# Sums over the states in a selective scan: two blocks at a time in four column tiles, with smaller rings of buffers

## The chip, the cores and the metric

The kernel runs on one core of a Trainium2 chip. A core has five engines that work side by side, each through its own queue of instructions in order: TensorE (PE in the profile, its weight loads PEld), VectorE (DVE), ScalarE (ACT), GpSimd (POOL) and SyncE (SP), which here issues nearly all DMAs. They wait for each other through semaphores. The metric is the time of one launch on the device in microseconds (us), median of several runs.

## What is computed

The input is a batch of 32 images of 96 channels and 56 x 56 pixels, all in float32. First comes a block of a depthwise 7 x 7 convolution, a layer norm over the channels, two dense layers with a GELU between them, and a residual. Then come two layers of a state space model over the 3136 pixels of an image as a sequence, each of this form:

```python
xs, z = jnp.split(layernorm(seq) @ in_w, 2, axis=-1)       # 192 channels each
xc = silu(causal_conv(xs) + conv_b)
dt, Bm, Cm = split(xc @ xproj_w)                            # 6, 16 and 16 columns
delta = softplus(dt @ dt_w + dt_b)
dA  = exp(delta[..., None] * A)                             # tokens x 192 x 16 states
dBx = delta[..., None] * Bm[:, :, None, :] * xc[..., None]
h   = associative_scan(dA, dBx)                             # h = dA * h_before + dBx
y   = einsum('blds,bls->bld', h, Cm) + Dp * xc              # the sum over the 16 states
seq = seq + (y * silu(z)) @ out_w
```

A fusion with a pooled vector, a batch norm over all images and a residual end it. The change concerns the line of `y`: the sum over the 16 states of each channel.

## The kernel before, in words

**Stages.** An image is cut into 4 chunks of 784 tokens. One chunk in one layer is a stage, 256 in all; the two layers alternate, the second one chunk behind the first. A stage has 24 steps: block `j` (0 to 5) of 32 channels, and in it group `g` (0 to 3) of 4 states. A step's tile has 128 partitions, 4 states x 32 channels, and 784 tokens.

**A step.** ScalarE makes the factor `exp(delta * A)` (L836). For blocks 0, 1, 3 and 4, TensorE spreads the product `delta * xc` of 32 channels onto 128 partitions in PSUM (the spread, L851, once a block, ahead of the block's first step), VectorE multiplies it by B (L878) and scans (L885). For blocks 2 and 5, the constant `POOLED`, GpSimd does that product from a copy in SBUF instead (L862), some steps in advance. Then GpSimd multiplies the states by C (L889) into the tile `da`, and TensorE adds up the four states of a tile with a matrix of ones, `ssum` (L922), in float32. Such a matmul has 128 rows and 32 columns of the array, and the profile has two passes of it.

**The sums.** The tokens of a tile are two halves `a` of 392, and the result `y` of two blocks shares one PSUM tile of 128 partitions: row `64 * a + 32 * (j % 2)`. Each of these four places is a column tile of the array of its own. A step's sum fills two of them. For each pair of blocks a matmul with a diagonal matrix opens the accumulation with `D * xc` (L916), and when the pair is done VectorE multiplies `y` by the gate `z` (L903) and so frees the one buffer of `y`.

**The order of the work** is written by hand. Each engine runs its instructions in the order in which the program issues them. A loop over steps `n` issues the exponentials of a later step, the scan of `n`, at the end of a block the spread of `n + 1`, and the sums of step `n - 3` (`LAG = 3`). Two of the steps (`LATE`) shift the sums by one, so that the opening matmul of the next pair comes behind the gate. All the other work of neighbouring stages is put into numbered slots of the same loop (`put`, `run`), by lists of (slot, piece): the norms (centring L355, mean L365, the multiplies L419 and L575), dense layers and projections (L424, L439, L443, L587, L614, L644), the output projection of the stage before (L750, L756), and in stages 2 to 145 seven taps twice of the convolution of later images (L506). A piece with `True` is issued just ahead of the scan. In the loop of a slot, the spread comes first, the sums next, the pieces last.

**Buffers.** Tiles of one tag form a ring: a new tile takes the place of an old one, and its first writer waits until the old one's last reader is done. The ring `da` of 11 holds the exponentials of blocks 0, 1, 3 and 4 and the products of blocks 2 and 5; each is overwritten by the product with C and read by the sum. B and C of a stage are four tiles `bc`, one a group, in a ring of 8: two stages. Each is loaded by four DMAs (L632), which spread a row over 32 partitions.

Of the kernel before, what the change touches and what calls it, by code (L numbers as in the profile page):

```python
# [34 lines left out]
F32 = mybir.dt.float32  # L35
# [13 lines left out]
NG = 4  # L49
# [3 lines left out]
CH = L // NCH  # L53
HC = CH // 2
# [7 lines left out]
def convnext_mamba_kernel(  # L62
# [31 lines left out]
    nc = tc.nc  # L94
# [34 lines left out]
    for a in range(2):  # L129
        r = slice(64 * a, 64 * a + 64)  # L130
# [8 lines left out]
    ssum = const.tile([128, 32], F32, name="ssum")  # L139
# [55 lines left out]
    for i in range(2):  # L195
# [39 lines left out]
        for s in range(4):  # L235
            r = slice(32 * s, 32 * s + 32)
# [11 lines left out]
    for k in range(2):  # L248
        t = const.tile([C + 1, 3 + CH], F32, name=f"hn{k}", tag=f"hn{k}")
        nc.vector.memset(t[C : C + 1, :], 1.0)  # L250
        hns.append(t)
        t = const.tile([C + 1, HC], F32, name=f"hz{k}", tag=f"hz{k}")
# [7 lines left out]
    with tc.tile_pool(name="cc", bufs=1) as cc, tc.tile_pool(name="cx", bufs=3) as cx, tc.tile_pool(  # L260
        name="cp", bufs=6, space=PSUM
# [4 lines left out]
        for dh in range(7):  # L266
            m = cc.tile([R2, R2], F32, name="m", tag="m", bufs=2)
# [25 lines left out]
        for i in range(3):  # L293
            t = cc.tile([R2, 7, R2], F32, name=f"band{i}", tag=f"band{i}")
            nc.gpsimd.memset(t, 0.0)
            bands.append(t)
            t = cc.tile([R2, b0, W + 6], F32, name=f"xpad{i}", tag=f"xpad{i}")
            nc.gpsimd.memset(t, 0.0)
            xpads.append(t)
        for p in range(C // 2):  # L300
# [13 lines left out]
            for lo in range(0, b0, GB):  # L314
                n = min(GB, b0 - lo)
                ps = cps.tile([R2, GB * W], F32, name="ps")
                for dw in range(7):
                    nc.tensor.matmul(
                        ps[:, 0 : n * W], T[:, dw, :], xp[:, lo : lo + n, dw : dw + W],
                        start=(dw == 0), stop=(dw == 6),  # L320
# [8 lines left out]
    with ExitStack() as main:  # L329
        wp = main.enter_context(tc.tile_pool(name="wp", bufs=2))  # L330
# [12 lines left out]
        def tok(a):  # L343
            return slice(a * HC, (a + 1) * HC)

        def rows(a):
            return slice(64 * a, 64 * a + 64)
# [193 lines left out]
        def prep(S):  # L541
# [52 lines left out]
            def silu(name, bias):  # L594
                def piece():
                    t = wp.tile(
                        [128, NQ, HC], F32, name=name, tag=name, bufs=3 if name == "z" else 2
                    )
                    for q in range(NQ):
                        nc.scalar.activation(  # L600
                            t[:, q, :], v["x", q][:, 0:HC], AF.Silu,
                            bias=0.0 if bias is None else bias[:, q, :],
                        )
                    if name == "z":
                        exp_ln_tables()
                    setattr(S, name, t)

                return piece
# [18 lines left out]
            def load_bc(gs):  # L627
                def piece():
                    for g in gs:
                        t = wp.tile([128, 2, CH], F32, name="bc", tag="bc", bufs=8)  # L630
                        for s in range(4):
                            nc.sync.dma_start(  # L632
                                t[32 * s : 32 * s + 32],
                                v["bd"][4 * g + s :: NS, :].partition_broadcast(32),
                            )
                        S.bcs.append(t)

                return piece
# [54 lines left out]
            def load_d4(j):  # L693
# [11 lines left out]
            start = [  # L705
                (-18, load), (-12.9, center), (-11.9, square), (-11.8, halo), (-11.6, mean),
                (-11.2, root), (-9, True, norm),
            ]
            t = (-7.6, -7.5, -6.5, -6, 0, 0.1, 1, 2.3, 3.1, 3.4, 4)
            if S in (stages[2], stages[-1]):  # L710

                start = [
                    (10.3, center), (10.4, square), (10.5, halo), (10.9, mean), (11, root),
                    (12, norm),
                ]
                t = (12, 12, 13, 13, 14, 14, 15, 16, 17, 18, 19)
            elif S is stages[3]:

                start = [
                    (-18, load), (-4.5, center), (-4.4, square), (-4.3, halo), (-3.5, mean),  # L720
                    (-3, root), (-2, norm),
                ]
                t = (0, 0, 0.1, 0.2, 0.3, 1, 2, 3.3, 4.1, 4.4, 5)
            t = [k + 0.1 for k in t]
# [4 lines left out]
                (t[6], silu("xc", d["cb"])), (t[6] + 0.1, project(0, wz, (0,), 3, 0)),  # L729
                (t[6] + 0.1, project(1, wz, (0,), 3, 0)), (t[6] + 0.1, project(2, wz, (0,), 3, 0)),  # L730
                (t[6] + 0.2, silu("z", None)), (t[7], dbl), (t[8], dbl_out),
                (max(10.2, t[8] + 1.2), load_bc((0, 1))), (max(13.2, t[8] + 2.2), load_bc((2, 3))),
                (t[9], dt), (t[10], softplus),
                (max(16.9, t[10] + 1.5), product(0, 2)), (max(18.3, t[10] + 3.1), store_u(0)),
                (25.2, product(2, 3)), (26.3, store_u(1)),
# [66 lines left out]
        NSTEP = 2 * NQ * NG  # L802

        ring = wp.tile([128, NG, CH], F32, name="h", tag="h", bufs=1)
        LAG = 3
        LATE = (4, 12)
# [8 lines left out]
        for i, b, c in order:  # L815
            S = Stage()
# [5 lines left out]
        def wide():  # L822

            return pu.tile([128, 1024], F32, name="w", tag="w", bufs=2)

        def exps(n):

            m, r = divmod(n, NSTEP)
            if m == len(stages):
                return  # L830
            S, j, g = stages[m], r // NG, r % NG
            if j in POOLED:
                e = wide()[:, 0:CH]
            else:
                e = S.da[j, g] = wp.tile([128, CH], F32, name="da", tag="da", bufs=11)
            nc.scalar.activation(e, S.d4[j], AF.Exp, scale=S.d["A"][:, j, g : g + 1])  # L836
            S.e[j, g] = e

        def lead(n):

            return 1 if n % NSTEP // NG in POOLED else 2

        def spread(n):

            m, r = divmod(n, NSTEP)
            if m == len(stages) or r // NG in POOLED:
                return
            S, j = stages[m], r // NG
            S.u4 = wide()
            for a in range(2):  # L850
                nc.tensor.matmul(  # L851
                    S.u4[:, 512 * a : 512 * a + HC], sel[rows(a), j % 2, :],
                    S.u[rows(a), j // 2, :], start=True, stop=True,
                )

        def pooled(m, j, g):


            def piece():
                S = stages[m]  # L860
                t = S.da[j, g] = wp.tile([128, CH], F32, name="da", tag="da", bufs=11)
                nc.gpsimd.tensor_tensor(t, S.us[j], S.bcs[g][:, 0, :], ALU.mult)  # L862

            return piece
# [26 lines left out]
        def keep_state(n):  # L891

            m, r = divmod(n, NSTEP)
            S, j, g = stages[m], r // NG, r % NG
            if g % 2 == 1 and S.c < NCH - 1:
                nc.scalar.copy(  # L896
                    S.d["st"][:, j, g - 1 : g + 1].unsqueeze(2), ring[:, g - 1 : g + 1, CH - 1 : CH]
                )

        def gate(n):  # L900
            m, r = divmod(n, NSTEP)
            S, q = stages[m], r // NG // 2
            nc.vector.tensor_tensor(S.z[:, q, :], S.y[:, 0:HC], S.z[:, q, :], ALU.mult)  # L903

        def add_up(n):

            if n < 0:
                return
            m, r = divmod(n, NSTEP)
            S, j, g = stages[m], r // NG, r % NG  # L910
            q = j // 2
            if j % 2 == 0 and g == 0:
                if j == 4:
                    gate(n - 1)
                S.y = py.tile([128, 512], F32, name="y", tag="y")
                nc.tensor.matmul(  # L916
                    S.y[:, 0:HC], S.d["D"][:, q, :], S.xc[:, q, :], start=True, stop=False
                )
            da = S.da.pop((j, g))
            for a in range(2):  # L920
                r0 = 64 * a + 32 * (j % 2)
                nc.tensor.matmul(  # L922
                    S.y[r0 : r0 + 32, 0:HC], ssum, da[:, tok(a)],
                    start=False, stop=(g == NG - 1),
                )


        slots, within = {}, {}
# [6 lines left out]
        def run(n, where):  # L935
            for _, piece in sorted(where.pop(n, ()), key=lambda p: p[0]):
                piece()
# [24 lines left out]
        with tc.manual_schedule(  # L962
            engines={ET.PE, ET.Activation, ET.DVE, ET.Pool, ET.SP}
        ):
            end = len(stages) * NSTEP
            for n in range(-2 * NSTEP, 0):
                run(n, within)
                run(n, slots)
            spread(0)
            for n in range(2):  # L970
                exps(n)
            for n in range(end + NSTEP):
                if n < end:
                    for k in (1, 2):
                        if lead(n + k) == k:
                            exps(n + k)
                    if n:
                        keep_state(n - 1)
                    scan(n)
                    if n % NG == NG - 1:  # L980
                        spread(n + 1)
                if n < end + LAG:
                    if n % NSTEP in LATE:
                        add_up(n - LAG - 1)
                    if n % NSTEP + 1 not in LATE:
                        add_up(n - LAG)
                elif n == end + LAG:
                    gate(end - 1)
                if n >= end:
                    run(n, within)  # L990
                run(n, slots)
# [4 lines left out]
    with tc.tile_pool(name="sp", bufs=1) as sp:  # L996
        n = B * NCH
# [21 lines left out]
    with tc.tile_pool(name="fin", bufs=4) as fin:  # L1019
        for b in range(B):  # L1020
            for a in range(2):
# [3 lines left out]
                r = fin.tile([C, 2 * CH], F32, name="fr")  # L1025
# [63 lines left out]
```

## Time and profile before

| | before |
|---|---|
| time, median of 3 runs | 17439.26 us (17436.45 to 17451.02) |
| profiled execution, span | 17444.6 us |
| scans L885, busy | 11076.0 us over four forms of operands, 6144 of them, 1766 to 1844 ns each |
| products L878 of VectorE, busy | 3996.2 us, 976 ns each |
| multiplies by C L889 of GpSimd, busy | 11267.2 us, 1856 ns each |
| products L862 of GpSimd, busy | 3819.1 us, 1865 ns each |
| sums L922 of TensorE, busy | 5147.1 us, 24576 passes |
| bytes moved | 2346 MB, 135 GB/s on average |

How to read it: busy time is the time in which an engine worked on instructions of a group; passes of matmuls overlap, so their mean duration times their number is more than the busy time. The waits of an engine are the times in which it stood idle, put down to what it waited for last. The windows and timelines show short stretches, with the clock granted to TensorE as a share of full speed (1.00 or 0.50).

### The profile page before, as it was taken

Reading aid. Unit: us, or ns where it says so; the run is one execution under the profiler, and the core shown is the slowest. Engines: PE = TensorE matmul, PEld = TensorE weight load, DVE = VectorE, ACT = ScalarE, POOL = GpSimd, SP = SyncE. Lnnn points to the kernel's source line nnn. Section 1 sums busy time; section 2 is a strip of 40 time slices with the busy share of each in tenths; the row PEclk is TensorE's granted clock in tenths of the full one; section 3 lists DMA queues with packets and bytes.
Section 4 is the critical chain, followed back from the end, with each engine's and each line's share of the span. In section 5 each row is a group of like instructions: output and inputs, shape, how many; then the busy total and the mean of one; then the engine's idle time right before and its main releaser. Section 6 shows DMA issues by size and latency. Waiting matters only on the chain. (4 is left out here: it accounts for less than half of the span.)

```text
span 17444.6 us, 217495 instructions
## 1 busy us (share of the span) xinstructions
PE 15502.9 (89%) x67992; PEld 5472.5 (31%) x67992; DVE 16064.8 (92%) x12345; ACT 11460.0 (66%) x18647; POOL 15605.6 (89%) x8737
## 2 busy tenths in 40 slices
PE   7799999999999999999999988888888888888870
PEld 5233333333333333333333322222222222222220
DVE  7499999999999999999999999999999999999994
ACT  1566766666666666666666666666666666666653
POOL 0499999999999999999999999999999999999991
PEclk9799999999999999999999999999999999999985
DMA  4355555555555555555555555555555555555548
GB/s 101 87 141 138 141 138 136 138 140 139 140 135 139 138 139 139 136 137 138 139 140 138 134 126 130 127 125 126 126 129 128 125 126 126 129 127 124 127 115 276
DMA packets 1421981, 2346.44 MB, mean 135 GB/s; under 512 B 629958, under 2 KB 793586, under 8 KB 1420820
## 3 DMA queue, kind: packets, MB, share of 16 engines
q1 hardware_dynamic: 1413652, 2294.00, 53.7%
q10 hardware_dynamic: 7168, 38.54, 0.6%
q8 instruction: 536, 8.78, 0.2%
q14 instruction: 625, 5.12, 0.1%
HBM read 1929.11 MB, written 402.41 MB: 134 GB/s over the span
## 5 line engine op out<-in xcount | busy, mean ns | idle before, releaser
L889 POOL TENSOR_TENSOR da<-h,bc 128x784 f32<-128x784 f32 x6144 | 11267.2, 1856 | 855.6 <-DVE h L885 734.9
L885 DVE TENSOR_TENSOR_SCAN h<-da,st,w 128x784 f32<-128x784 f32 x3072 | 5664.5, 1844 | 326.4 <-ACT st L896 8.6
L922 PE MATMUL y<-da,ssum 128*32 128x392 f32 x24576 | 5147.1, 542 | 407.2 <-POOL da L889 403.2
L878 DVE TENSOR_TENSOR w<-w,bc 128x784 f32<-128x784 f32 x4096 | 3996.2, 976 | 300.9 <-PE w L851 132.7
L862 POOL TENSOR_TENSOR da<-us,bc 128x784 f32<-128x784 f32 x2048 | 3819.1, 1865 | 2.3 <-DMA us<-uu 2.3
L836 ACT ACTIVATE da<-d,A 128x784 f32<-128x784 f32 x4096 | 3757.4, 941 | 43.1 <-DMA d<-dd 27.3
L836 ACT ACTIVATE w<-d,A 128x784 f32<-128x784 f32 x2048 | 1878.3, 918 | 2635.0 <-DVE h L885 2285.8
L885 DVE TENSOR_TENSOR_SCAN h<-w,st,da 128x784 f32<-128x784 f32 x1536 | 2712.2, 1827 | 5.9 <-ACT w L836 4.8
L587 PE MATMUL ps<-hn,wx 97*64 97x392 f32 x12288 | 2265.9, 503 | 7.4 <-DVE hn L575 7.4
L922 PEld LDWEIGHTS y<-da,ssum 128*32 128x32 f32 x24576 | 1094.8, 115 | 3681.1 <-issue 2141.1
L885 DVE TENSOR_TENSOR_SCAN h<-da,w 128x784 f32<-128x784 f32 x1024 | 1827.0, 1784 | 109.1 <-ACT st L896 4.3
L851 PE MATMUL w<-u,sel 64*128 64x392 f32 x4096 | 1026.5, 580 | 655.0 <-DVE h L885 654.0
L587 PEld LDWEIGHTS ps<-hn,wx 97*64 97x64 f32 x12288 | 793.7, 137 | 1434.5 <-issue 1117.3
L666 POOL TENSOR_TENSOR u<-dl,xc 128x784 f32<-128x784 f32 (+1 forms) x512 | 737.5, 1440 | 564.1 <-ACT dl L652 564.1
L916 PE MATMUL y<-xc,D 128*128 128x392 f32 x1536 | 802.2, 608 | 257.1 <-DVE z L903 249.4
L506 PE MATMUL ps<-xpad,band 112*112 112x224 f32 (+1 forms) x4032 | 1003.0, 358 | 0.0
L351 ACT ACT_TABLE_LOAD x759 | 973.8, 1283 | 14.3 <-PEq L1076 0.8
L885 DVE TENSOR_TENSOR_SCAN h<-w,da 128x784 f32<-128x784 f32 x512 | 872.3, 1766 | 0.0
L360 ACT ACTIVATE sq<-ps 96x392 f32<-96x392 f32 x768 | 340.7, 490 | 797.3 <-PE ps L355 448.9
L506 PEld LDWEIGHTS ps<-xpad,band 112*112 112x112 f32 x4032 | 583.7, 175 | 832.5 <-issue 770.0
L644 PE MATMUL ps<-dbl,dtw 6*64 6x392 f32 x3072 | 685.7, 509 | 99.6 <-ACT dbl L622 99.6
L851 PEld LDWEIGHTS w<-u,sel 64*128 64x128 f32 x4096 | 327.9, 196 | 1255.6 <-DVE h L885 1096.3
(124 smaller groups left out, 14444.6 us busy)
## 6 DMA issues: line engine op xcount, KB each, us to landing
bc<-bd SPq DMA_DIRECT2D x4096, 196.0 KB, 5.3
d<-dd SPq DMA_DIRECT2D x6144, 98.0 KB, 2.9
us<-uu SPq DMA_DIRECT2D x2048, 98.0 KB, 2.2
dd<-dl SPq DMA_DIRECT2D x512, 294.0 KB, 3.8
uu<-u SPq DMA_DIRECT2D x1024, 49.0 KB, 1.6
band<-band_d SPq DMA_DIRECT2D x144, 343.0 KB, 3.6
cv<-conv_d SPq DMA_DIRECT2D x256, 147.0 KB, 2.5
xin<-in_x SPq DMA_DIRECT2D x128, 294.0 KB, 4.2
```

Of the source, the lines that this page charges most:

```text
L351: nc.scalar.preload_act_table_set("natural_log_exp_and_others")
L506: nc.tensor.matmul(v["ps"][0:R2, 0 : (last - first) * W], v["band"][:, dw, :], xpad[:, first:last, dw : dw + W], start=(dw == 0), stop=(dw ...
L587: nc.tensor.matmul(v["x", q][rows(a), 0:HC], weights[:, k, 64 * q : 64 * q + 64], v["hn"][:, o : o + HC], start=(k == 0), stop=(k == last),)
L666: nc.gpsimd.tensor_tensor(S.u[:, lo:hi], v["dl"][:, lo:hi], S.xc[:, lo:hi], ALU.mult)
L836: nc.scalar.activation(e, S.d4[j], AF.Exp, scale=S.d["A"][:, j, g : g + 1])
L851: nc.tensor.matmul(S.u4[:, 512 * a : 512 * a + HC], sel[rows(a), j % 2, :], S.u[rows(a), j // 2, :], start=True, stop=True,)
L862: nc.gpsimd.tensor_tensor(t, S.us[j], S.bcs[g][:, 0, :], ALU.mult)
L878: nc.vector.tensor_tensor(halves(db), S.u4.rearrange("p (a b) -> p a b", a=2)[:, :, 0:HC], halves(S.bcs[g][:, 0, :]), ALU.mult,)
L885: nc.vector.tensor_tensor_scan(ring[:, g, :], S.e.pop((j, g)), db, 0.0 if c == 0 else d["st"][:, j, g : g + 1], ALU.mult, ALU.add,)
L889: nc.gpsimd.tensor_tensor(da, ring[:, g, :], S.bcs[g][:, 1, :], ALU.mult)
L916: nc.tensor.matmul(S.y[:, 0:HC], S.d["D"][:, q, :], S.xc[:, q, :], start=True, stop=False)
L922: nc.tensor.matmul(S.y[r0 : r0 + 32, 0:HC], ssum, da[:, tok(a)], start=False, stop=(g == NG - 1),)
```

## The change

The sums of two blocks are done together. In the odd block of a pair, the sum of step `n` takes the tile of the same group of the even block with it: four matmuls in four column tiles instead of two in two, and none during the even block. The opening matmul with `D * xc` moves to the odd block's first sum, the `LATE` shift falls away, and the gate of the second pair is issued at step 19, where it stood before.

The tiles of the even block must live longer, until the odd block's sum. For that the ring `da` of 11 becomes two: 8 tiles for the exponentials of blocks 0, 1, 3 and 4, and a ring `dp` of 6 for the products of blocks 2 and 5. The room comes from B and C: 6 tiles instead of 8, so that the loads of the groups 2 and 3 are issued in slots 22 and 23 of the stage before, where the tiles of the groups 0 and 1 come free, instead of slot 13.

It is meant to make better use of the array[...] and to take half of the bursts of sums off TensorE's queue.

```diff
-                        t = wp.tile([128, 2, CH], F32, name="bc", tag="bc", bufs=8)
+                        t = wp.tile([128, 2, CH], F32, name="bc", tag="bc", bufs=6)
...
-                (max(10.2, t[8] + 1.2), load_bc((0, 1))), (max(13.2, t[8] + 2.2), load_bc((2, 3))),
+                (max(10.2, t[8] + 1.2), load_bc((0, 1))), (22, load_bc((2,))), (23, load_bc((3,))),
...
-                e = S.da[j, g] = wp.tile([128, CH], F32, name="da", tag="da", bufs=11)
+                e = S.da[j, g] = wp.tile([128, CH], F32, name="da", tag="da", bufs=8)
...
-                t = S.da[j, g] = wp.tile([128, CH], F32, name="da", tag="da", bufs=11)
+                t = S.da[j, g] = wp.tile([128, CH], F32, name="da", tag="dp", bufs=6)
...
         def add_up(n):
 
-            if n < 0:
+            m, r = divmod(n, NSTEP)
+            if n < 0 or r // NG % 2 == 0:
                 return
-            m, r = divmod(n, NSTEP)
             S, j, g = stages[m], r // NG, r % NG
             q = j // 2
-            if j % 2 == 0 and g == 0:
-                if j == 4:
-                    gate(n - 1)
+            if g == 0:
                 S.y = py.tile([128, 512], F32, name="y", tag="y")
                 nc.tensor.matmul(
                     S.y[:, 0:HC], S.d["D"][:, q, :], S.xc[:, q, :], start=True, stop=False
                 )
-            da = S.da.pop((j, g))
-            for a in range(2):
-                r0 = 64 * a + 32 * (j % 2)
-                nc.tensor.matmul(
-                    S.y[r0 : r0 + 32, 0:HC], ssum, da[:, tok(a)],
-                    start=False, stop=(g == NG - 1),
-                )
+            das = [S.da.pop((j - 1, g)), S.da.pop((j, g))]
+            for jj in range(2):
+                for a in range(2):
+                    r0 = 64 * a + 32 * jj
+                    nc.tensor.matmul(
+                        S.y[r0 : r0 + 32, 0:HC], ssum, das[jj][:, tok(a)],
+                        start=False, stop=(g == NG - 1),
+                    )
...
+                    if n % NSTEP == 19:
+                        gate(n - LAG - 1)
                 if n < end + LAG:
-                    if n % NSTEP in LATE:
-                        add_up(n - LAG - 1)
-                    if n % NSTEP + 1 not in LATE:
-                        add_up(n - LAG)
+                    add_up(n - LAG)
```

## The prediction

> **What bounds the kernel now.** I read the page's busy shares first, then VectorE's own waits, then the clock and the timelines of single stages. A stage is one block of 784 tokens in one layer: 24 steps, numbered 0 to 23 (block j = step // 4); 24 to 28 are the first steps of the next stage. Its 256 stages fill nearly the whole span.
>
> ```profile
> PE 15502.9 (89%) x67992; PEld 5472.5 (31%) x67992; DVE 16064.8 (92%) x12345; ACT 11460.0 (66%) x18647; POOL 15605.6 (89%) x8737
> ```
>
> Three engines look full, so this line alone decides nothing. TensorE is the first to rule out: from 10240 us on the convolution taps (L506) are done, its busy share falls from 95% to 87% (8917.81 of 9380 us before, 1746.78 of the 2000 from 12000 us), and a stage still takes 64.2 us against 64.0 (distance of the first scans of neighbouring stages). GpSimd: its multiply L889 lags the scan L885 by 2 to 4.4 us, its own duration of 1.86 included, less than two steps, and at steps 6, 12, 14 and 16 it waits for the scan; it has a little room. VectorE has none: between 860 and 10240 us its waits add up to some 130 us in 9380. Only they can be won. VectorE's waits, with the convolution and without:
>
> ```profile
> DVE w L878 <- PE w L851: 106.3, 152, 2.2
> DVE z L903 <- PE y L922: 23.3, 20, 1.5
> ...
> DVE hz L419 <- ACT ps L372: 92.2, 70, 2.3
> ```
>
> With the convolution VectorE waits for the spread L851, which comes late because TensorE's queue is full. Without it, it waits for a norm, and the reason is TensorE's clock (columns: PE, PEld, DVE, ACT, POOL busy, then the clock):
>
> ```profile
> 13495.39:13498.81 3.42, 0.85 (x4) 0.14 (x4) 3.42 (x3) 2.19 (x4) 3.42 (x3) 1.00 0.55 132
> 13498.81:13502.22 3.41, 2.31 (x5) 0.90 (x6) 3.31 (x3) 3.19 (x5) 3.41 (x3) 0.50 1.02 236
> 13502.22:13505.63 3.41, 3.41 (x7) 1.55 (x6) 3.38 (x4) 0.00 (x0) 3.04 (x3) 0.50 1.04 226
> 13505.63:13509.05 3.42, 3.42 (x15) 1.26 (x14) 3.12 (x3) 1.59 (x4) 3.42 (x3) 1.00 1.05 235
> ```
>
> [...] A window with TensorE 25% busy is followed by half clock, one with 68% keeps half clock, a full one gives full clock back. Counted over the trace: at full clock all 72 windows under 30% busy are followed by half clock, none of 551 between 40 and 70%; at half clock none of 65 windows under 70% leads back, nearly all of 249 over 90% do. Stage 61 shows what half clock costs one run of matmuls, from the spread of step 16 to the last sum (L922) that the gate (L903) of step 19 needs:
>
> ```profile
> 4598.72 0.93 PE L851 MATMUL w<-u,sel 64*128 64x392 f32 x4 [1.80 <-DVE h L885]
> 4600.41 4.29 PE L424 MATMUL ps<-hz,w_sb 97*128 97x392 f32 x6
> 4614.40 0.85 PE L922 MATMUL y<-da,ssum 128*32 128x392 f32 x4
> ...
> 4615.30 0.57 DVE L903 TENSOR_TENSOR z<-y,z 128x392 f32<-128x392 f32 x1 [1.14 <-PE y L922]
> ```
>
> The run takes 16.53 us with 6.83 us at half clock; in stage 200 at full clock 13.30 (13512.18 to 13525.48). So each us at half clock adds 0.475 us, and the gate waits for whatever exceeds 16.53 - 1.14 = 15.4 us. The second run that matters, in stages 200 and 201:
>
> ```profile
> 13524.63 0.85 PE L922 MATMUL y<-da,ssum 128*32 128x392 f32 x4
> 13533.37 0.93 PE L851 MATMUL w<-u,sel 64*128 64x392 f32 x4 [0.86 <-DVE h L885]
> 13544.63 0.93 PE L851 MATMUL w<-u,sel 64*128 64x392 f32 x4
> ...
> 13547.07 0.98 DVE L878 TENSOR_TENSOR w<-w,bc 128x784 f32<-128x784 f32 x1
> ```
>
> The spread of step 24 begins when scan 22 ends; TensorE then works without a pause to the spread of step 28, done at 13545.56, and VectorE takes it at 13547.07: 1.5 us to spare.
>
> [...]
>
> **The change, part by part.**
>
> Sums. Before: 24 bursts a stage of two matmuls, one every 0.78 us in a queue (13541.75 to 13542.53, L922 to L614). After: 12 bursts of four, at steps 7-10, 15-18 and 23-26. If four tiles run side by side a burst costs the same 0.78; if in pairs, 0.78 + 0.66 (eight passes take 1.51 against 0.85 for four). I take 0.78, since the two tiles already run freely beside each other. TensorE saves 12 x 0.78 = 9.4 us a stage, all at steps 3-6, 11-14 and 19-22. VectorE's and GpSimd's orders are the same, so no busy time leaves them.
>
> What this wins. With the convolution the queue ahead of the spreads of steps 0 and 12 gets shorter by four bursts each (4 x 0.78 = 3.1 us), against waits of 2.2 us at most: 106 us go. Without it, the norm at step 14 now stands behind the spread and the centring alone, no longer behind L916 and two bursts (13505.54 to 13507.78, 2.2 us), against a mean wait of 1.3: 92 us go. With the 23 us of the gate, which I work out anew, 222 us in all.
>
> What this loses: idle TensorE at steps 13-15 and 19-22, thus half clock on the two runs above. The D matmul (L916) also moves into them, from steps 12 and 19 to steps 15 and 23: 0.83 us (start to next start). Where the idle time is over 5 us, half clock is certain[...]: 2.9 to 6.3 us into the run as the grid falls, so 1.4 to 3.0 us are added.
> - Gate of step 19, with the convolution: the mean matmuls (L365) end some 5.7 us before the spread of step 16. 13.30 + 0.83 + (1.4 to 3.0) - 15.4 = 0.1 to 1.7, on average 0.9 us x 144 stages = 130 us.
> - The same without convolution: the centring itself is at half clock and ends later, idle 3.2 us; no half clock in a third of the stages, one window in half of them (wait about 0.4), nearly two in the rest (1.7). Average 0.5 us x 110 = 55 us.
> - Spread of step 28, without convolution: from the end of L587 after the last sum to the spread of step 24 some 5 us are idle (no burst, no tap). To spare 1.5 - 0.83 + 0.2 (a wait for GpSimd in the run that falls away) = 0.9. Wait 0.5 to 2.1, on average 1.2 us x 110 = 130 us. With the convolution the taps of steps 18-22 fill this idle time to about 2 us: nothing.
>
> Rings, at nothing. Queued behind a waiting exponential (L836) on ScalarE would be all later ones, and the scans after them; but a tile of the ring of 8 is freed by a sum at least three steps before its next writer (step 28's by the sum of 20 in the burst of step 23), and ScalarE is 66% busy. On GpSimd the multiplies queue behind L862; its product of step 16 needs the sum of step 12, which TensorE does 3 to 4 us after scan 14 ends, while GpSimd reaches it 8.5 us after.
>
> B and C. With 6 tiles the loads for g = 2 and 3 wait for GpSimd's multiplies of steps 20 and 21, 3.5 us behind the scan. Queued behind them on SyncE are a tap store and the later loads of d4, band and image; none is needed for several steps. From the end of that multiply to the product of step 26 there are 7.8 us (8.3 with the convolution); four issues 0.47 us apart and 4.4 us for the last to land make 6. I charge nothing; the upper bound, a landing of 7.4 us (slowest in a hundred), would be 1 us in few stages.
>
> Sum: -222 + 130 + 55 + 130 = +93 us; averages over the grid are the weak point and partly double-counted (a late gate also moves later deadlines), so I take +80: 17439 + 80 = 17519 us.
>
> **The rivals.**
> - The clock holds or the runs have more room: all 222 us are won, 17217 us; with half of the new waits 17375. For it: TensorE loses 9 us of work a stage, and VectorE waits for TensorE in most of its named waits. Against it: stage 61's 1.14 us at the very gate. Chance 0.27.
> - Exchange of waits, as worked out: 17519, from 17440 to 17620. Chance 0.58.
> - Slower than that: four tiles run in pairs. Each run then gets 4 x 0.66 = 2.6 us more, 5.3 us a stage, 1350 us: 18870. Or B and C late by 1 us a stage: 17775. Against it: passes of two tiles start together, and the loads have 1.8 us to spare. Chance 0.15 together.
>
> **How the numbers follow.** Likeliest: 17519. The range 17260 to 17680 takes in the exchange, most of the first rival (partial gains) and the mildest late loads, and leaves out about 2 in 10. Faster by over 0.2% (under 17404): the first rival and a little of the second, 0.30. Within 0.2%: 0.18. Slower: 0.52.
>
> **What would show it.** Right: the clock at 0.50 far more often, TensorE's busy share well under 89%, the waits L878 <- L851 with convolution and L419 <- L372 nearly gone, and in their place L903 waiting for the sums and L878 for the spread of step 4. L921 bursts of eight passes take 0.85 us. Wrong: bursts of 1.5 us, L878 waiting for bc, ScalarE or GpSimd waiting for sums, or no waits of the gate although TensorE idles.

## The result, and the profile after

The changed kernel takes 17932.6 us (median; 17900.79 to 17960.62) against 17437.85 us before in the same session: 1.0282 times, 95% interval 1.0264 to 1.0300, slower by 495 us. The direction was forecast, the size was not (17519 us, range to 17680).

The busy times of the changed kernel, from its page:

```profile
PE 14647.6 (82%) x67992; PEld 5293.3 (30%) x67992; DVE 16088.6 (90%) x12345; ACT 11435.6 (64%) x18647; POOL 15610.8 (87%) x8737
```

TensorE's busy time fell by 855 us, although half clock covers 4531 us instead of 1863 (860 to 17000 us). The sums alone fell from 5147.1 to 3350.3 us; the spreads, the opening matmuls and others took longer. VectorE and GpSimd have the same work to within 25 us, so what was added is waiting. VectorE's own waits say for what; the first two lines are from 860 to 10500 us, with the convolution, the next three from 10500 to 17700 us, without. The last two are those of the kernel before from 10500 to 17300 us (columns: us in total, times, longest):

```profile
DVE w L878 <- PE w L851: 205.1, 179, 3.5
DVE z L903 <- PE y L921: 176.7, 146, 1.9
...
DVE w L878 <- PE w L851: 172.9, 132, 2.5
DVE z L903 <- PE y L921: 126.6, 102, 3.4
...
DVE hz L419 <- ACT ps L372: 7.0, 39, 0.3
...
DVE w L878 <- PE w L851: 10.8, 5, 4.8
DVE z L903 <- PE y L922: 3.4, 1, 3.4
```

The wait for the norm (L419 <- L372) is gone, as forecast. In its place VectorE waits for TensorE at the gate and at the spreads, 681 us where the same four lines of the kernel before add up to 144. L921 are the sums and L914 is the opening matmul, which stood in lines 922 and 916 before.

Stage 200 shows the run of matmuls up to the gate of step 19. Three stretches of time of it (TensorE's busy time first, the clock third from the end):

```profile
13864.30:13867.71 3.41, 0.46 (x2) 0.00 (x0) 3.38 (x4) 3.35 (x7) 3.41 (x2) 1.00 0.09 22
13867.71:13874.54 6.83, 6.02 (x16) 2.04 (x17) 6.59 (x8) 2.60 (x3) 5.57 (x4) 0.50 0.22 62
13874.54:13881.37 6.83, 6.83 (x40) 2.51 (x39) 6.49 (x6) 4.84 (x6) 6.12 (x4) 1.00 0.07 17
```

After a window with TensorE 0.46 of 3.41 us busy come 6.83 us at half clock. The timeline of TensorE and VectorE in that stage (start, us, what):

```profile
13868.52 1.68 PE L851 MATMUL w<-u,sel 64*128 64x392 f32 x4 [3.76 <-DVE h L885]
13870.12 1.67 PE L914 MATMUL y<-xc,D 128*128 128x392 f32 x2
13871.73 1.54 PE L921 MATMUL y<-da,ssum 128*32 128x392 f32 x8
...
13884.67 0.87 PE L921 MATMUL y<-da,ssum 128*32 128x392 f32 x8
...
13885.63 0.57 DVE L903 TENSOR_TENSOR z<-y,z 128x392 f32<-128x392 f32 x1 [1.67 <-PE y L921]
13891.58 1.68 PE L851 MATMUL w<-u,sel 64*128 64x392 f32 x4 [4.57 <-DVE h L885]
13904.94 0.93 PE L851 MATMUL w<-u,sel 64*128 64x392 f32 x4
...
13905.92 0.98 DVE L878 TENSOR_TENSOR w<-w,bc 128x784 f32<-128x784 f32 x1 [0.81 <-PE w L851]
```

TensorE idles 3.76 us, then runs from 13868.52 to 13885.54, 17.02 us. The prediction's sum gives 13.30 + 0.83 + 0.475 x 6.02 us of half clock = 16.99. It holds beyond this stage: over stages 150 to 249, a straight line through the lengths of this run against their half clock has 14.15 us where there is none, and adds 0.476 us for each us. TensorE idles again, 4.57 us, and the spread of the next stage's step 4 is late. The bursts of four column tiles are what was hoped: eight passes take 0.87 us at full clock, where four took 0.85.

The same by place of the stage. These are sums of VectorE's gaps over 0.15 us in the trace, per stage, over stages 20 to 139 with the convolution and 150 to 249 without; each profile is of one execution:

| kernel | with: step 0 | step 4 | step 12 | gate, step 19 | without: step 4 | norm, step 14 | gate, step 19 |
|---|---|---|---|---|---|---|---|
| before | 0.55 | 0 | 0.24 | 0.15 | 0 | 0.92 | 0 |
| after | 0.03 | 0.60 | 0.73 | 1.17 | 1.57 | 0.07 | 1.22 |
| e1, rings alone | 0.53 | 0 | 0.22 | 0.15 | 0 | 0.98 | 0 |
| e2, fillers in all idle places | 0.68 | 0.05 | 0.36 | 0.60 | 0.09 | 0 | 0.26 |
| e3, opening early | 0 | 0 | 0.54 | 0.94 | 0.64 | 0.19 | 0.44 |
| e4, gate late | 0 | 0 | 0.31 | 0 (0.84) | 0.55 | 0.07 | 0 (0.54) |
| e5, fillers at 13 and 14 | 0.01 | 0.62 | 0.41 | 0.08 | 1.33 | 0.15 | 0.92 |
| e6, opening early and gate late | 0 | 0 | 0.34 | 0 (0.60) | 0.57 | 0.20 | 0 (0.19) |
| e7, e6 and fillers | 0 | 0 | 0.17 | 0 | 0 | 0 | 0 |
| e8, fillers at 4 to 6 | 0.03 | 1.55 | 0.34 | 1.51 | 1.65 | 0 | 1.27 |

In brackets: a wait of the scan of step 20 for ScalarE instead. Two waits have no column: without the convolution, the spread of step 0 in e2 (0.81) and that of step 16 in e5 (0.32). After against before this is 1.59 us a stage with the convolution and 1.94 without; the distance of the first scans of neighbouring stages grew from 64.02 to 65.76 and from 64.18 to 66.12 us. 1.74 x 144 + 1.94 x 110 = 464 of the 495 us; where the rest arises was not worked out.

### The profile page after: what moved, and what is told of

Read it like the earlier page. It is cut to its first block, busy times and chain, and to the rows that moved or that the text cites. A ratio compares the mean times of both kernels' runs of the same rounds, so it can differ in the third digit from the quotient of the medians.

```text
span 17899.1 us, 218250 instructions
## 1 busy us (share of the span) xinstructions
PE 14647.6 (82%) x67992; PEld 5293.3 (30%) x67992; DVE 16088.6 (90%) x12345; ACT 11435.6 (64%) x18647; POOL 15610.8 (87%) x8737
## 4 chain that ended last, share of the span: by engine, by line
PE 20%; DVE 18%; issue 4%; ACT 3%; DMA 3%; POOL 2%; SPq 0%; DVEq 0%; POOLq 0%; ACTq 0%
DVE h L885 14%; PE ps L587 5%; PE y L921 4%; DVE w L878 4%; PE w L851 3%; PE y L914 2%; PE ps L355 2%; PE ps L614 1%; ACT w L836 1%; POOL da L889 1%; PE ps L424 1%; DMA fr<-x_d 1%; POOL da L862 1%; PE ps L443 1%; DMA out_y<-fo 1%
## 5 line engine op out<-in xcount | busy, mean ns | idle before, releaser
L921 PE MATMUL y<-da,ssum 128*32 128x392 f32 x24576 | 3350.3, 577 | 237.8 <-POOL da L889 235.3
L851 PE MATMUL w<-u,sel 64*128 64x392 f32 x4096 | 1326.4, 733 | 2109.8 <-DVE h L885 2109.8
L921 PEld LDWEIGHTS y<-da,ssum 128*32 128x32 f32 x24576 | 632.0, 117 | 2512.7 <-issue 1852.4
L851 PEld LDWEIGHTS w<-u,sel 64*128 64x128 f32 x4096 | 409.1, 239 | 2700.8 <-DVE h L885 1539.6
L914 PE MATMUL y<-xc,D 128*128 128x392 f32 x1536 | 1141.6, 841 | 23.1 <-DVE z L903 23.1
L432 ACT ACTIVATE gl<-ps,b_sb 128x392 f32<-128x392 f32 x768 | 451.9, 588 | 1060.6 <-PE ps L424 1024.7
L506 PE MATMUL ps<-xpad,band 112*112 112x224 f32 (+1 forms) x4032 | 856.9, 345 | 0.0
L600 ACT ACTIVATE xc<-ps,cb 128x392 f32<-128x392 f32 x768 | 423.9, 585 | 651.3 <-PE ps L587 648.3
L365 PE MATMUL ps<-sq,mean_m 96*96 96x392 f32 x1536 | 686.1, 580 | 149.6 <-ACT sq L360 149.6
```

Of the source, the lines that this page charges most:

```text
L506: nc.tensor.matmul(v["ps"][0:R2, 0 : (last - first) * W], v["band"][:, dw, :], xpad[:, first:last, dw : dw + W], start=(dw == 0), stop=(dw ...
L851: nc.tensor.matmul(S.u4[:, 512 * a : 512 * a + HC], sel[rows(a), j % 2, :], S.u[rows(a), j // 2, :], start=True, stop=True,)
L914: nc.tensor.matmul(S.y[:, 0:HC], S.d["D"][:, q, :], S.xc[:, q, :], start=True, stop=False)
L921: nc.tensor.matmul(S.y[r0 : r0 + 32, 0:HC], ssum, das[jj][:, tok(a)], start=False, stop=(g == NG - 1),)
```

## The experiments

The theory: TensorE is left idle, its clock falls to half, and the two runs of matmuls that follow the idle times, made longer by the opening matmul, come late. Rivals: the smaller rings and late loads of B and C; runs that are too long at any clock; a TensorE that is behind as a whole.

The diffs are shortened, some to their sense. Four kernels first, run beside each other and the kernel before (17439.84 us there).

**e1: the rings alone.** The kernel before with this of the change:

```diff
-  bc: bufs=8, load_bc((2, 3)) at 13.2;  da: one ring of 11
+  bc: bufs=6, load_bc((2,)) at 22, load_bc((3,)) at 23;  da: bufs=8, dp: bufs=6
```

> The kernel before with the smaller rings alone (da 8, dp 6, bc 6, late loads of B and C); sums as before. Theory 1 (half clock of TensorE in the two runs of matmuls, made longer by the opening matmul): the rings cost nothing, 17438 us within 0.2%, and no wait for bc over 10 us in all. Rival (buffers): B and C late or exponentials held up by the rings carry a good part of the 495 us lost, 17600 to 17930.

17435.52 us, ratio 1.0000 (0.9991 to 1.0008). With the old order of the sums, rings and loads cost nothing. In the changed kernel VectorE waits 10.9 us in all for B and C and GpSimd 69.5 (46.6 before), and e7 below is fast with the same rings. So the 495 us come from the new order of the sums.

**e2: fillers in every idle place of the changed kernel.**

```diff
+  WARM = {4: 2, 5: 2, 6: 2, 11: 2, 12: 1, 13: 1, 14: 1, 19: 2, 20: 2, 21: 2, 22: 2}
+  for _ in range(4):          # at step n, behind GpSimd's product of step n - WARM[n]
+      nc.tensor.matmul(bank[:, HC:512], D, da[:, 0:512 - HC], start=True, stop=True)
```

> The changed kernel with filler matmuls in the idle steps 4-6, 11-14 and 19-22 (four of 120 columns a step, each behind a product of GpSimd, into unused columns of y's bank); they add some 9 us of TensorE's work a stage and compute nothing that is used. Theory 1: the clock stays full, the gate of step 19 and the spreads of steps 4 and 12 are in time, 17200 to 17420 us, faster than before although TensorE does more. Rival (the runs are too long at any clock, since bursts and the opening matmul are packed into them): no gain, 17930 or slower by the fillers' work.

17611.18 us, ratio 1.0098 (1.0082 to 1.0115). Work of TensorE was added and 321 us were won against the changed kernel, so the rival that expected no gain falls, though this kernel stays slower than the one before. The gain fell short of the forecast: by the table the fillers ahead of step 24 make its spread late themselves (0.68 us with the convolution), and half clock was not gone: the mean granted clock of this execution was 0.944 (0.851 in the changed kernel).

**e3: the opening matmul at steps 4, 12 and 19, behind the gates.**

```diff
-            if g == 0:
-                S.y = py.tile(...); nc.tensor.matmul(S.y, D, xc, start=True, stop=False)
+                    if n % NSTEP in (4, 12, 19):
+                        opening(n, (4, 12, 19).index(n % NSTEP))
```

> The changed kernel with the opening matmul back at steps 4, 12 and 19, behind the gates. Theory 1: 0.83 us less in the run before the gate of step 19 and in that before the spread of step 28, about 325 us in all where the waits are that long, 17600 us; the clock still falls to half. Rival (clock alone counts): the idle times stay, under 100 us are won. Rival (buffers): no change, 17930.

17575.1 us, ratio 1.0077 (1.0062 to 1.0092): 357 us won, where 325 were expected. The matmul of 0.83 us also fills idle time in the place it goes to: with the convolution the mean idle time ahead of step 24 is 1.64 us instead of 2.35, half clock at step 23 goes from 46% of the time to none, and the wait of step 4, 0.60 us, with it.

**e4: the gate of the second pair at step 22.**

```diff
-                    if n % NSTEP == 19:
-                        gate(n - LAG - 1)
+                    if n % NSTEP == 22:
+                        gate(n - LAG - 4)
```

> The changed kernel with the gate of the second pair issued at step 22 instead of 19. Theory 1: its wait of 1.2 us a stage goes, 305 us of 495, 17630 us; the spread of step 4 stays late. Rival (TensorE is behind as a whole, and the gate is only where VectorE meets it first): the wait comes back at the next spreads, over 17850 us.

17529.06 us, ratio 1.0053 (1.0038 to 1.0068): 403 us won, 100 more than the gate's waits and than forecast; the spread of step 4, which was to stay late, is in time with the convolution. VectorE's waits with the convolution, from 860 to 10300 us:

```profile
DVE h L885 <- ACT w L836: 122.3, 143, 1.1
DVE w L878 <- PE w L851: 44.0, 38, 2.2
```

The gate's 177 us are gone, and the spreads' waits fell from 205 to 44 us too, although no matmul was moved. A gate that waits makes VectorE late, so that TensorE idles longer ahead of step 24 (2.35 us on average in the changed kernel with the convolution, 1.14 here), and the clock falls there (half clock for 46% of step 23, none here). A smaller new wait came up: the exponential of step 20, on ScalarE. The gate's wait went as the theory has it, and the waits turn out to feed each other.

Then three that separate the clock from the order of the queue (before: 17429.96 us).

**e5: fillers ahead of the first run alone.**

```diff
+  WARM = {13: (1, 8), 14: (1, 6)}     # step: (steps back, number of matmuls)
```

> The changed kernel with fillers in two places alone: 8 matmuls of 120 columns at step 13 and 6 at step 14, each behind the product of the step before; they compute nothing that is used. They add TensorE's work ahead of the run before the gate of step 19 and touch no other. Theory 1 (half clock in that run makes the gate late): half clock at steps 14 to 16 gone, the gate's wait of 1.2 us a stage gone, about 17530 us as with the gate issued later. Rival (the run is too long by what is packed into it): the wait stays at 1.2 us or grows by the fillers, 17930 us or more.

17702.81 us, ratio 1.0158 (1.0143 to 1.0173). With the convolution the answer is clean: half clock at steps 14 and 15 fell from 82% and 91% of the time to 0 and 2%, and the gate's wait from 1.17 to 0.08 us, with 14 matmuls added ahead of it. Without the convolution it is not. Half clock went here too (1% of step 15), but TensorE was at half clock ahead of the fillers (76% of step 13), they began late, and the run started 2.28 us after the end of scan 14, where it starts after 0.06 us in the changed kernel (0.99 us in e5 with the convolution). The gate kept 0.92 us. The spread of step 4 kept its wait, since e5 does not fill the idle time ahead of step 24. So the total missed the 17530 us.

**e6: opening at 4, 12 and 20 and the gate at 20.**

```diff
+                    if n % NSTEP == 20:
+                        gate(n - 5)
+                    if n % NSTEP in (4, 12, 20):
+                        opening(n, (4, 12, 20).index(n % NSTEP))
```

> The changed kernel with the opening matmul at steps 4, 12 and 20 and the gate of the second pair at step 20: both edits that won time alone. Theory 1: no wait of the gate, the spread of step 4 up to 0.6 us late without convolution and that of step 12 about 0.5 us with it, still half clock: 17400 us. Rival (the two edits win the same time): 17520 us.

17451.65 us, ratio 1.0009 (1.0002 to 1.0016). Together the two edits win 481 us, 78 more than the later gate alone, not the 760 of both: each had already removed part of the other's waits, and 17400 us was missed. Half clock stays (4178 us of it from 860 to 17000 us, against 4531 in the changed kernel and 1863 before), and with it these waits, 860 to 10300 us first, then 10300 to 17300:

```profile
DVE h L885 <- ACT w L836: 84.6, 49, 2.2
DVE w L878 <- PE w L851: 50.0, 38, 2.5
...
DVE w L878 <- PE w L851: 64.4, 64, 3.3
```

**e7: e6 and fillers.** They are added into y with zero weights and change nothing in it:

```diff
+  WARM = {4: (2, 4), 5: (2, 4), 6: (2, 4), 13: (1, 8), 14: (1, 6), 20: (2, 4), 21: (2, 4)}
+      nc.tensor.matmul(y[:, 0:120], zeros, da[:, 0:120], start=False, stop=False)
```

> The same with fillers at steps 4 to 6, 13, 14, 20 and 21 (zero weights, added to y without effect). Theory 1: with the clock kept full the waits of all three places go, 17230 to 17330 us, clearly below the kernel before. Rival (idle TensorE is not what costs time): not below e6, slower by the fillers' queueing.

17261.35 us, ratio 0.9903 (0.9889 to 0.9918). Its page, and its waits in the two stretches (L853 is the spread, L880 the product):

```profile
PE 15326.9 (89%) x85400; PEld 7370.0 (43%) x85400; DVE 16059.0 (93%) x12346; ACT 11477.8 (67%) x18647; POOL 15598.8 (90%) x8737
```

```profile
DVE w L880 <- PE w L853: 22.6, 31, 1.5
DVE w L880 <- DMA bc<-bd: 8.6, 19, 0.8
...
DVE w L880 <- PE w L853: 13.0, 11, 6.8
```

From e6 to e7 only matmuls that compute nothing were added, 17408 passes and 883 us of TensorE's busy time, and 190 us went away, with half clock down from 4178 to 1572 us. This is the strongest evidence for the theory. It is also a version that beats both kernels: 671 us under the changed one, 169 under the one before. ScalarE's wait went with the rest; the likely link, not tried by itself, is the GELU ahead of it on ScalarE, which waits for L424 in the first run.

Two places were left: step 12 with the convolution, and the kernel before itself (before: 17443.93 us).

**e8: fillers at steps 4, 5 and 6 of the changed kernel.**

```diff
+  WARM = {4: (2, 4), 5: (2, 4), 6: (2, 4)}
```

> The changed kernel with fillers at steps 4, 5 and 6 alone (four of 120 columns each). Theory 1: the output projection of the stage before (L756), behind the first sums, then runs at full clock, so the spread of step 12 with convolution comes in time: its wait of 0.73 us falls to about 0.2, 75 us are won, 17855 us; the gate and the spread of step 28 stay as late as they are. Rival (TensorE's queue is too full at steps 7 to 11): the wait stays or grows, 17930 us or more.

17984.41 us, ratio 1.0314 (1.0299 to 1.0330). The place behaves as expected: step 12's wait falls from 0.73 to 0.34 us. But nothing is won in all: step 4 rises from 0.60 to 1.55 us and the gate from 1.17 to 1.51, as half clock rose at step 23 (from 46% of the time to 93%) and at step 15 (91% to 100%); that was not foreseen. (The interval of the ratio meets that of the changed kernel, 1.0264 to 1.0300, so that e8 is slower than it is likely, not certain; the profile of e8 is of its slowest execution, 18008.6 us.) The idle time ahead of step 24 did not grow: 2.35 us on average in both. What differs is where it falls on the grid of windows. In the changed kernel it begins in the second half of a window in 51 of 120 stages, so that less than half of a window is idle, and in none of these half clock follows; of the other 69, 59 are followed by it. In e8 it begins in the first half in 119 of 120, and half clock follows in all 119. Two stages there last 38.98 windows, so that the idle times keep their places on the grid; in the changed kernel it is 38.52. How much of this is the fillers' doing and how much chance of the length of a stage, no run tried.

**e9 and e10: the kernel before, fillers without the convolution.** Both keep its sums of one block at a time.

```diff
+  WARM = {8: (1, 5), 9: (1, 3)}       # e9
+  WARM = {8: (2, 8), 9: (2, 2)}       # e10
+      for r0 in (32, 96):
+          nc.tensor.matmul(y[r0:r0 + 32, 0:196], zeros, da[:, 0:196], start=False, stop=False)
```

> The kernel before (sums of one block at a time, its own rings) with fillers at steps 8 and 9 in the stages without convolution alone (pairs of 32 columns of zero weights, 5 and 3 of them). Theory 1 holds for it too: its wait of 0.92 us for the norm at step 14 comes from half clock at steps 10 to 12, so it goes, 100 us in all, 17340 us. Rival (the norm is late because of the sums ahead of it): no change, 17435.

17562.21 us, ratio 1.0071 (1.0055 to 1.0088). VectorE's waits from 10300 to 16900 us:

```profile
DVE w L880 <- PE w L853: 216.4, 101, 3.9
```

The norm's 92 us are gone, but the spread of step 12, which stands behind the fillers, is late by 2.1 us a stage; they wait for a product of GpSimd that comes too late (290 us in these 101 stages). That alone gives the norm time, so the run settles nothing.

> As e9, the kernel before with fillers without convolution, but these stand behind older products (8 pairs at step 8, 2 at step 9, each two steps back), so that TensorE is done with them before the spread of step 12 is asked for. Theory 1: half clock at steps 10 to 12 gone and the spread in time, so the norm's wait of 0.92 us goes and nothing takes its place: 17340 us. Rival (the norm is late because of the sums ahead of it): the wait at step 14 stays, 17435 us or more.

17336.22 us against 17435.03, ratio 0.9939 (0.9923 to 0.9956), where 17340 was expected. The same stretch:

```profile
DVE z L905 <- PE y L924: 12.4, 10, 1.5
DVE w L880 <- PE w L853: 8.0, 6, 2.3
```

L905 is the gate and L924 the sums here. VectorE waits neither for the norm nor for the spread of step 12, and the sums stand ahead of the norm as before. So the kernel before already lost about 100 us to half clock. The changed kernel lost the same wait by another way: two bursts and the opening matmul no longer stand ahead of the norm, while half clock still covers 72% of step 11 and 49% of step 12 (89% and 70% before, none in e10). So the wait could be removed by either, and the order of the queue had a part in it.

## Why the prediction was right or wrong

**Right.** VectorE's waits were the only thing to win or lose; the rings and the loads of B and C cost nothing (e1); four tiles run as fast as two (eight passes in 0.87 us, four in 0.85; the passes of two tiles already started 7 ns apart before); the norm's wait went (0.92 to 0.07 us) and step 0's too (0.55 to 0.03); the exchange of waits for half clock at the gate and at step 28 is what happened. Each us of half clock costs the 0.475 us read from stage 61, as the runs of matmuls in the result show (0.476).

**Wrong: the sizes.** Forecast +93 us before rounding, measured +495. The range was left on the side of the third rival, but for neither of its reasons: bursts of eight passes took 0.87 us, not 1.5, and VectorE waited 10.9 us in all for B and C. By the terms of the sum, in us over all stages (table above times 144 or 110):

| term | forecast | measured |
|---|---|---|
| spreads of steps 0 and 12, with convolution | -106 | -75 + 71 = -4 |
| norm of step 14, without | -92 | -94 |
| gate of step 19, with (net of before) | +130 - 23 | +147 |
| gate of step 19, without | +55 | +134 |
| spread of step 28, with | 0 | +86 |
| spread of step 28, without | +130 | +173 |

The measured terms add up to 442 us. Four steps failed.

First, "The taps of steps 18-22 fill this idle time to about 2 us: nothing." The idle time was 2.35 us on average, partly because the late gate holds VectorE back, and that was enough for half clock in 46% of step 23. The prediction's own stage 61 had shown such a case: 1.80 us of idle time, a window 47% busy, and then half clock:

```profile
4596.85:4600.26 3.41, 1.61 (x10) 0.45 (x8) 3.41 (x6) 3.36 (x6) 2.63 (x2) 1.00 1.04 224
4600.26:4607.09 6.83, 6.83 (x16) 2.56 (x16) 6.42 (x6) 4.51 (x6) 5.73 (x4) 0.50 0.64 140
```

So a window need not be idle, and the count "none of 551 between 40 and 70%" does not hold. Counted again in windows between the times at which the clock's records change, 860 to 17300 us, all 65 windows under 30% fall, and 60 of 108 between 40 and 50%; none of 264 between 50 and 70% does. At half clock 340 of 453 windows over 90% lead back, not nearly all. The prediction had also noted that a late gate moves later deadlines, and then took it for a relief. e4 shows that it is a cost.

Second, "106 us go". Step 12 became worse. The idle steps 4 to 6 were not among the places the prediction looked at for half clock, since the kernel before is at half clock there too (71% of step 4 with the convolution). But the sums that stood at steps 3 to 6 are gone, and half clock, which with the convolution covered 8% of step 6 and none of step 7, now covers 57% and 43% of them and reaches into the output projection. Stage 66 of the changed kernel:

```profile
5007.11 2.93 PE L750 MATMUL ps<-seq,eye 96*96 96x392 f32 x4
5009.97 3.96 PE L756 MATMUL ps<-z,ow 64*96 64x392 f32 x12
...
5019.66 0.93 PE L851 MATMUL w<-u,sel 64*128 64x392 f32 x4
...
5020.64 0.98 DVE L878 TENSOR_TENSOR w<-w,bc 128x784 f32<-128x784 f32 x1 [3.48 <-PE w L851]
```

At full clock the twelve passes of L756 took 2.22 us (median of the 256 stages of the kernel before); here, at a mean granted clock of 0.55, they take 3.96, the taps follow late, and VectorE waits 3.48 us for the spread, the longest of these waits. In e8 fillers at just these steps halve the wait.

Third, the gate without the convolution: "no half clock in a third of the stages". The idle time was near the 3.2 us assumed (2.90 on average), but the clock was often at half already when it began (53% of step 13), and no third of the stages was spared: half clock covered 4.9 us of the run on average, and all 100 gates were late, by 1.22 us instead of 0.5.

Fourth, smaller: the averages over the window grid were low, 1.17 for 0.9 us and 1.57 for 1.2. They rest on the author's estimate that half clock lasts 2.9 to 6.3 us of a run, which at 0.475 us for each is 1.4 to 3.0 us; no count of the prediction showed it. One likely reason is in the counts of the last section: in the changed kernel 206 of 218 windows between 80 and 90% busy kept half clock.

The rival that all 222 us are won comes near once the clock is kept in more places and the gate gets room: e7 gains 169 us over the kernel before. But e10 shows that fillers help the kernel before too, 99 us, and no run gave it fillers in the stages with the convolution. So how much of e7's lead is due to the new order of the sums is not shown.

## What to carry to other kernels

Before taking work off TensorE, look in the trace for the places where the work kept its clock up, and price the next run of matmuls at half clock. Here each us of half clock added 0.476 us, and an idle time of 2.35 us on average was mostly enough for it where it began in the first half of a window of 3.41 us (59 of 69 stages). Half clock, lateness and idle time fed each other along a loop here (e4), so a cure in one place alone won nothing (e8: 17984 us against 17933), while order and fillers together won (e7: 17261). Give a consumer room (the gate one step later, the opening matmul earlier: 481 us in e6) before making its producer faster.

## What the runs showed of the hardware

More matmuls made the kernel faster: TensorE busy 89% in e7 and 83% in e6, 17261 against 17452 us. The traces of the kernel before and of the changed one hold two values of the clock, 1.00 and 0.50. From 860 to 17300 us it changes 681 and 1441 times, and any two changes stand a whole multiple of 3.41 us apart. What follows is counted in windows of that grid in this stretch. All idle times of TensorE over 5 us that began at full clock, 6 before and 80 in the changed kernel, were followed by half clock. In the changed kernel all 380 windows at full clock with TensorE under 40% busy are followed by half clock; at half clock all 354 windows under 80% busy stay, and so do 206 of the 218 between 80 and 90%, but only 79 of 788 above. Shifting the windows by a tenth moves some counts, above all those between 80 and 90%; at full clock all under 30% still fall, and at half clock all under 60% stay.

Some windows over 70% busy at full clock also fall to half: 196 in the kernel before, 237 in the changed one. They are windows with the small matmuls L644, 6 rows of the array by the trace (6*64): with the time of L644 left out, no window over 70% busy falls in either kernel (none of 3428 and none of 2548). In e7 half clock stays at steps 4 and 5, where L644 runs (66% and 46% of the time with the convolution). Why L644 differs, no run tried.
